# The context stage of a cross-attention kernel in written issue order, with the first group's keys and values taken together

## Chip, cores and metric

The kernel runs on one core of a Trainium2 chip. The metric is the device time of one execution in microseconds (us). The measurements are of whole executions; the profile is of one of them.

## The reference

Inputs are `x` (32 x 512 x 640), a context `ctx_2048` (32 x 77 x 1024) and weights `wq` (640 x 640), `wk` and `wv` (1024 x 640), `wo` (640 x 640) with a bias. Cut to what reaches the output:

```python
q = heads(x @ wq)                      # 20 heads of 32
k = heads(ctx @ wk); v = heads(ctx @ wv)    # 77 tokens per batch
p = softmax(einsum('bhqd,bhkd->bhqk', q, k) / sqrt(32))
out = merge(einsum('bhqk,bhkd->bhqd', p, v)) @ wo + bias + x
```

The reference also has key and value projections for object, other and image tokens. They take the context's tokens beyond the 77th, and there are none, so nothing of them reaches the output.

## The kernel before

Every float32 product is made of three products of halves: an operand is split into a high part (a copy rounded to `fp32r`, on ScalarE, ACT) and a low part (the operand less the high part, on VectorE, DVE, or on GpSimd, POOL), and `PAIRS` lists high x high, high x low and low x high. The helper `split` (L104 for the high part, L105 for the low) serves weights, context, keys and values, so many operations have its lines and are told apart by tile.

**The context stage.** The 32 x 77 = 2464 context tokens are worked in five groups of 512 (the last has 416). For a group, `load_context` loads its tokens (tile `cs`, L144, issued on SyncE's queue, SP), `context` transposes one chunk of 128 channels in 32 x 32 blocks on DVE (tile `craw`, L153) and splits it (tile `ct`, 9 buffers). There are `NK` = 8 such chunks. `keys` (L164) adds three matmuls of one chunk `k` for one block `j` of 128 key columns into a bank of PSUM (`pk`); there are `NC_` = 5 blocks, so a group has 120 matmuls for keys and, in `context_values` (L192, tile `pv`), 120 for values. A finished block of keys is split (`ks`, two buffers) and stored into `k_dram` (L177 and L179, issued on POOL, for the last group on SP). A finished block of values is transposed (`vt`, L200, one buffer), split (`vs`, two buffers) and stored into `v_dram` (L205, on SP).

`split_weights` loads one or two chunks of a weight (tile `wraw`, two buffers, L114) and splits them (`wk_s`, `wv_s`, `wq_s`). In group 0 it takes wk chunk by chunk with the context; wv is loaded after that, behind the keys; wq follows in group 1 and wo, which is stored split in `wo_dram`, in group 2. Twelve matmuls on a tile of zeros (`warm`, L237) run on TensorE (PE) before the first load has landed. The tile of zeros also fills the tail of `v_dram`.

In the last group the keys go block by block. Its values go later, as fillers beside the first slots of the main loop, and the first batch of `x` is loaded (`load_x`, tile `xs`), transposed (`transpose_x`) and split (`split_x`, tile `xt`, L228 and L229) in its time.

**Order.** Up to there, the order of the instructions on each engine is the tile framework's: its scheduler orders the program by a timeline that it works out itself, from the data flow, the buffers and its own costs. From `with tc.manual_schedule` near the end of the function on, the order on each engine is the written one. DMAs issued by one engine stand in that engine's order, too: a load whose buffer is not yet free holds up all that is issued behind it.

**The main loop.** It has N = 160 slots (32 batches x 5 blocks of 4 heads): `queries` (tile `pq`, L353), `split_q` (`qt`, L364 to L370), `scores` (`sc`, L388; `nm`, L396), exponentials (L406), normalisation and a transpose through DRAM, values (`pa`, L480) and the output projection (`po`, L510). It reads the keys back from `k_dram` (tiles `kb`, `kc`) and the values from `v_dram` (`vb`). Slots 0 and 1 have the last group's values beside them, through `psv`.

## Time and profile before

| | us |
|---|---|
| median of 3 runs | 1971.68 |
| their range | 1971.13 to 1974.15 |
| the profiled execution | 1971.65 |
| its span, first to last instruction | 1969.2 |
| busy in it: PE / ACT / DVE / POOL | 1932.0 / 1592.9 / 1362.1 / 1020.6 |
| mean granted clock of TensorE | 0.994 |

The profiled execution's time exceeds its span by 2.45 us, which lie before the first and after the last instruction. In a row of a timeline the columns are the start and the duration in us, the engine, the line, the operation, the tile written and the tiles read, shapes, the number of instructions taken together, and in brackets the idle time ahead of them with what ended it. In a row of the chain of waits they are start, duration and what the time went to. PEld is the load of weights into TensorE, which overlaps matmuls; SPq and POOLq are the issue of DMAs by SyncE and GpSimd. PEclk is the clock that TensorE was granted as a share of full speed; the DMA share is the mean busy share of the core's 16 DMA engines.

### The profile page before, as it was taken

The page shows a single profiled execution, that of the slowest core. Times are in us where ns is not written, and L with a number is a line of the kernel's source. Part 1 is how long each engine was busy: PE and PEld are TensorE (multiplying, and loading weights), DVE is VectorE, ACT ScalarE, POOL GpSimd, SP SyncE. Part 2 cuts the span into 40 slices and gives each one's busy share as a digit, 9 for nine tenths or more (in the row PEclk, how much of TensorE's full clock was granted, in tenths as well). Part 3 has the DMA queues.
Part 4 walks back from the last instruction along what each step waited for, and adds up shares of the span by engine and source line. Part 5 has one row for each costly group of instructions (what it writes and reads, how often), then busy time and mean ns, then how long its engine had stood idle before and what let it go on. Part 6 is the DMA issues. An engine that isn't in the chain of part 4 may idle for free.

```text
span 1969.2 us, 37571 instructions
## 1 busy us (share of the span) xinstructions
PE 1932.0 (98%) x10652; PEld 1729.6 (88%) x10652; DVE 1362.1 (69%) x2166; ACT 1592.9 (81%) x6362; POOL 1020.6 (52%) x680
## 2 busy tenths in 40 slices
PE   7999998899999999999999999999999999999999
PEld 5788897789999999999999999999999999999998
DVE  4544345777777777777777777777777777777774
ACT  2422147889999999999999999999999999999993
POOL 0111143565555555565556665566556655555555
PEclk9999999899999999999999999999999999999999
DMA  9996478888888888888888888988888888888876
GB/s 188 247 215 125 97 147 188 226 224 231 221 231 228 222 228 226 231 229 223 224 228 234 218 227 224 234 227 227 227 224 225 222 227 223 226 225 227 231 192 188
DMA packets 600698, 423.49 MB, mean 215 GB/s; under 512 B 219792, under 2 KB 509358, under 8 KB 600494
## 3 DMA queue, kind: packets, MB, share of 16 engines
q1 hardware_dynamic: 596973, 410.61, 82.5%
q0 software_dynamic: 3520, 10.49, 2.0%
q8 instruction: 88, 1.44, 0.3%
q14 instruction: 117, 0.95, 0.2%
HBM read 245.61 MB, written 175.32 MB: 214 GB/s over the span
## 4 chain that ended last, share of the span: by engine, by line
PE 89%; DMA 5%; SPq 2%; issue 1%; ACT 1%; POOL 1%; DVE 1%; POOLq 0%; DVEq 0%; ACTq 0%
PE po L510 28%; PE pq L353 27%; PE pa L480 14%; PE sc L388 10%; PE pv L192 6%; PE pk L164 5%; DMA cs<-in_ctx_dram 1%; DMA wo_s<-wo_dram 1%; DMA wraw<-in_L_xattn_to_v_w_dram 1%; DMA k_dram<-ks 1%; SPq L435 1%; DMA raw<-pd 1%; DMA pd<-z 1%; SPq L144 0%; POOL pn L421 0%
## 5 line engine op out<-in xcount | busy, mean ns | idle before, releaser
L406 ACT ACTIVATE pn<-sc,nm 128x77 f32<-128x77 f32 x2560 | 797.3, 328 | 48.2 <-DVE nm L396 33.3
L421 POOL TENSOR_TENSOR pn<-pn,rs 128x1232 f32<-128x1232 f32 x160 | 364.4, 2277 | 641.9 <-DVE rs L416 629.7
L510 PE MATMUL po<-wo_s,at 128*128 128x320 f32 x3840 | 625.9, 312 | 0.1
L353 PE MATMUL pq<-xt,wq_s 128*128 128x512 f32 x2400 | 618.9, 398 | 2.4 <-DVE ks L105 1.2
L510 PEld LDWEIGHTS po<-wo_s,at 128*128 128x128 f32 x3840 | 565.0, 188 | 0.7 <-DVE xr L538 0.3
L406 ACT ACTIVATION_READ_ACCUMULATOR pn<-sc,nm 128x1 f32 x2560 | 529.1, 207 | 0.0
L396 DVE TENSOR_REDUCE nm<-sc 128x4 f32<-128x308 f32 x640 | 294.3, 460 | 315.9 <-PE sc L388 311.4
L353 PEld LDWEIGHTS pq<-xt,wq_s 128*128 128x128 f32 x2400 | 427.9, 189 | 79.7 <-POOL xt L229 2.4
L480 PE MATMUL pa<-pp,vb 128*128 128x512 f32 x1280 | 329.1, 399 | 2.2 <-POOL pp L466 2.0
L480 PEld LDWEIGHTS pa<-pp,vb 128*128 128x128 f32 x1280 | 243.2, 197 | 41.3 <-POOL pp L466 3.4
L428 DVE STREAM_TRANSPOSE z<-pn 128x1280 f32<-128x1280 f32 x160 | 241.1, 1507 | 27.5 <-POOL pn L421 16.9
L459 DVE TENSOR_TENSOR pp<-raw,pp 128x1024 fp32r<-128x1024 f32 x160 | 196.3, 1227 | 64.0 <-ACT pp L452 56.7
L466 POOL TENSOR_TENSOR pp<-raw,pp 64x512 fp32r<-64x512 f32 x160 | 210.6, 1317 | 48.6 <-ACT pp L458 29.1
L388 PEld LDWEIGHTS sc<-kc,qt 128*128 128x128 f32 x1280 | 212.0, 189 | 24.1 <-ACT qt L368 3.8
L370 DVE TENSOR_TENSOR qt<-pq,qt 64x512 fp32r<-64x512 f32 x320 | 214.6, 670 | 16.1 <-ACT qt L364 11.7
L229 POOL TENSOR_TENSOR xt<-xs,xt 128x512 fp32r<-128x512 f32 x160 | 204.1, 1293 | 40.8 <-DMA k_dram<-ks 32.8
L388 PE MATMUL sc<-kc,qt 128*128 128x154 f32 x1280 | 222.8, 255 | 2.2 <-DVE qt L370 2.1
L388 PE MATMUL sc<-kb,qt 128*128 128x308 f32 x640 | 195.8, 306 | 11.7 <-ACT pn L406 6.3
L503 POOL TENSOR_TENSOR xr<-xr,bias 128x640 f32<-128x640 f32 x128 | 200.9, 1571 | 9.7
L368 ACT CAST qt<-qt 64x512 fp32r<-64x512 f32 x320 | 198.0, 619 | 9.0
L452 ACT CAST pp<-raw 128x1024 fp32r<-128x1024 f32 x160 | 170.1, 1063 | 13.6 <-DMA raw<-pd 12.5
L104 ACT CAST at<-pa 128x512 fp32r<-128x512 f32 x160 | 94.5, 591 | 80.0 <-PE pa L480 79.7
(43 smaller groups left out, 1537.5 us busy)
## 6 DMA issues: line engine op xcount, KB each, us to landing
pd<-z SPq DMA_DIRECT2D x640, 160.0 KB, 3.5
raw<-pd SPq DMA_DIRECT2D x160, 512.0 KB, 4.3
xs<-in_x_dram SPq DMA_DIRECT2D x128, 320.0 KB, 6.1
xr<-in_x_dram SPq DMA_DIRECT2D x128, 320.0 KB, 3.7
out_dram<-xr SPq DMA_DIRECT2D x127, 320.0 KB, 3.0
raw<-pd SPq DMA_DIRECT2D x160, 128.0 KB, 4.4
v_dram<-vs SPq DMA_DIRECT2D x80, 128.0 KB, 3.1
kc<-k_dram SPq DMA_DIRECT2D x128, 57.8 KB, 4.1
```

What stands on the lines that cost most here:

```text
L229: low.tensor_tensor(parts[1], src, parts[0].bitcast(F32), ALU.subtract)
L353: nc.tensor.matmul(pqs[n], wq_s[:, k, a, j * P : (j + 1) * P], xts[b, k][:, c, :], start=(k == 0 and m == 0), stop=(k == NC_ - 1 and m == 2),)
L370: nc.vector.tensor_tensor(qt[r, 1 + w, :], pq[r], qt[r, 0, :].bitcast(F32), ALU.subtract)
L388: nc.tensor.matmul(sc[:, cols], qt[:, m, t * P : (t + 1) * P], keys_, start=(m == 0), stop=(m == 2),)
L396: nc.vector.tensor_reduce(nm, sc[:, :KCOLS].rearrange("p (h k) -> p h k", k=NKEY), AX.X, ALU.max, negate=True)
L406: nc.scalar.activation(pnb[n % 2][:, at, :NKEY], sc[:, i * NKEY : (i + 1) * NKEY], AF.Exp, bias=nm[:, i : i + 1], accum_out=sms[n][:, at : ...
L421: nc.gpsimd.tensor_tensor(pf, pf, rs.unsqueeze(2).to_broadcast([P, NQ * HPC, NKEY]), ALU.mult)
L428: nc.vector.transpose(z.rearrange("p b t j -> p t b j"), pn.rearrange("p (t h) k -> p t (h k)", t=NQ).rearrange("p t (b i) -> p t b i", i=Q),)
L466: nc.gpsimd.tensor_tensor(pp[64:, 4, :], raw[:64, 2, :], pp[:64, 4, :].bitcast(F32), ALU.subtract)
L480: nc.tensor.matmul(pas[n], vb[:, t, :, a], pp[:, c, :], start=(m == 0), stop=(m == len(PASSES) - 1),)
L503: nc.gpsimd.tensor_tensor(xrs[b, t], xrs[b, t], bias, ALU.add)
L510: nc.tensor.matmul(pos[b, t, h][:, :HALF], ats[b * NC_ + j][:, a, t * P : (t + 1) * P], wos[0][:, j, c, h * HALF : (h + 1) * HALF], start= ...
```

## The change

The whole context stage moves into the manual schedule, so that each engine takes its instructions in the written order. The functions are cut into parts that can be ordered separately: `load_weights` from `split_weights`, `transpose_context` from `split_context`, `split_keys` from `keys`, `values_of` and `split_values` from `context_values`.

In group 0, `first` takes a chunk of channels at a time: its transpose and split, the split of wk, 15 matmuls for the five blocks of keys, the split of wv and 9 matmuls for the first three blocks of values. The eight banks of PSUM hold five blocks of keys and three of values. Value blocks 3 and 4 follow as 48 matmuls. The loads go out by turns: context, wk and wv of one chunk (later of two), half of the first wk on ACT's queue and the first two chunks of wv on POOL's.

From group 1 on, a group's context is one tile of 8 chunks with one buffer, loaded by four DMAs of 512 KB when the group before it has been transposed. Its first chunk is transposed and split at value block 1 of the group before, the others before value block 4 is split. All five `split_keys` of a group come after its keys; the splits of wq and wo stand between `vt` and `vs`. `wraw` has three buffers, and wq is scaled in place.

In the last group the keys are taken in two rounds, blocks 0 to 2 and then 3 and 4, with `x` of batch 0 loaded ahead of the last value block of group 3 and its transposes and splits ahead of the last group's `ks`. The number of matmuls is the same, and the order of the main loop too.

```diff
--- before.py
+++ after.py
-    def split_weights(dst, w, k0, kn=1, permuted=True, scale=None):
-        raw = kvw.tile([P, 2, C], F32, tag="wraw", name="wraw", bufs=2)[:, :kn]
+    def load_weights(w, k0, kn, permuted=True, queues=(nc.sync,) * 4, tag="wraw"):
+        raw = kvw.tile([P, 2, C], F32, tag=tag, name="wraw", bufs=3 if tag == "wraw" else 2)
         if permuted:
             rows = w.rearrange("(q c i) n -> q i c n", q=4, i=Q)
-            for q in range(4):
-                nc.sync.dma_start(raw[q * Q : (q + 1) * Q], rows[q, :, k0 : k0 + kn])
+            for q, queue in enumerate(queues):
+                queue.dma_start(raw[q * Q : (q + 1) * Q, :kn], rows[q, :, k0 : k0 + kn])
         else:
-            nc.sync.dma_start(raw[:, 0], w[k0 * P : (k0 + 1) * P, :])
+            rows = w.rearrange("(c p) n -> p c n", p=P)
+            nc.sync.dma_start(raw[:, :kn], rows[:, k0 : k0 + kn])
         for k in range(kn):
-            part = raw[:, k]
-            if scale is not None:
-                part = kvw.tile([P, C], F32, tag="wscaled", name="wscaled", bufs=1)
-                nc.scalar.mul(part, raw[:, k], scale)
-            split(dst[:, k, 0, :], dst[:, k, 1, :], part)
+            wraws[id(w), k0 + k] = raw[:, k]
+    def split_weights(dst, w, k, scale=None):
+        part = wraws.pop((id(w), k))
+        if scale is not None:
+            nc.scalar.mul(part, part, scale)
+        split(dst[:, 0, :], dst[:, 1, :], part)
...
-    kvc = tc.alloc_tile_pool(name="kvc", bufs=3, side="right")
+    kvc = tc.alloc_tile_pool(name="kvc", bufs=1, side="right")
...
-    def load_context(g0, gn, k0, kn):
+    cts, pks, pvs, css, craws, wraws = ({} for _ in range(6))
+
+    def load_context(g, *counts):
+
+        g0, gn = GROUPS_KV[g]
         src = ehs_flat[g0 : g0 + gn, :].rearrange("(a j) (q u) -> q j a u", j=Q, q=4)
-        cs = kvc.tile([P, G // Q, 4 * Q], F32, tag="cs", name="cs", bufs=3)
-        for q in range(4):
-            nc.sync.dma_start(
-                cs[q * Q : (q + 1) * Q, : gn // Q, : kn * Q],
-                src[q, :, :, k0 * Q : (k0 + kn) * Q],
-            )
-        for k in range(kn):
-            css[g0, k0 + k] = cs[:, : gn // Q, k * Q : (k + 1) * Q]
-
-    def context(g0, gn, k):
-        raw = kvt.tile([P, G], F32, tag="craw", name="craw")
+        if g not in css:
+            css[g] = kvc.tile([P, G // Q, NK * Q], F32, tag="cs", name="cs"), [0]
+        cs, done = css[g]
+        for kn in counts:
+            cols = slice(done[0] * Q, (done[0] + kn) * Q)
+            for q in range(4):
+                nc.sync.dma_start(
+                    cs[q * Q : (q + 1) * Q, : gn // Q, cols], src[q, :, :, cols]
+                )
+            done[0] += kn
+
+    def transpose_context(g, k):
+        gn = GROUPS_KV[g][1]
+        craws[k] = kvt.tile([P, G], F32, tag="craw", name="craw")
         nc.vector.transpose(
-            raw[:, :gn].rearrange("p (a j) -> p a j", j=Q), css.pop((g0, k))
+            craws[k][:, :gn].rearrange("p (a j) -> p a j", j=Q),
+            css[g][0][:, : gn // Q, k * Q : (k + 1) * Q],
         )
+
+    def split_context(g, k):
+        gn = GROUPS_KV[g][1]
         ct = kvp.tile([P, 2, G], FPR, tag="ct", name="ct", bufs=9)
-        split(ct[:, 0, :gn], ct[:, 1, :gn], raw[:, :gn])
-        cts.append(ct)
-
...
-    def keys(g0, gn, j, k):
+        split(ct[:, 0, :gn], ct[:, 1, :gn], craws.pop(k)[:, :gn])
+        cts[g, k] = ct
+
+    def context(g, *ks):
+
+        transpose_context(g, ks[0])
+        for k in ks:
+            if k + 1 in ks:
+                transpose_context(g, k + 1)
+            split_context(g, k)
+
+    def context_product(held, tag, g, j, k, w, pool):
+        gn = GROUPS_KV[g][1]
         if k == 0:
-            pks[j] = psk.tile([P, G], F32, tag="ps", name="pk")
+            held[j] = pool.tile([P, G], F32, tag="ps", name=tag)
         for n, (a, c) in enumerate(PAIRS):
             nc.tensor.matmul(
-                pks[j][:, :gn],
-                wk_s[:, k, a, j * P : (j + 1) * P],
-                cts[k][:, c, :gn],
+                held[j][:, :gn],
+                w[:, k, a, j * P : (j + 1) * P],
+                cts[g, k][:, c, :gn],
                 start=(k == 0 and n == 0),
                 stop=(k == NK - 1 and n == 2),
             )
-        if k == NK - 1:
-            pk = pks.pop(j)
-            ks = kvt.tile([P, 2, G], FPR, tag="ks", name="ks")
-            split(ks[:, 0, :gn], ks[:, 1, :gn], pk[:, :gn])
-            engine = nc.gpsimd if g0 != GROUPS_KV[-1][0] else nc.sync
-            dst = k_dram.rearrange("(h r) c w n -> r c w h n", h=2)[:, j, :, :, g0 : g0 + gn]
-            engine.dma_start(dst[:, 0].bitcast(F32), ks[:64, :, :gn].bitcast(F32))
-            for half in range(2):
-                engine.dma_start(
-                    dst[:, 1, half].bitcast(F32), ks[64:, 1 - half, :gn].bitcast(F32)
-                )
-
-    xts, xss, xpool = {}, {}, []
-
-    def context_values(g0, gn, j, pool):
-
-
+
+    def keys(g, j, k):
+        context_product(pks, "pk", g, j, k, wk_s, psk)
+
+    def split_keys(g, j):
+        g0, gn = GROUPS_KV[g]
+        ks = kvt.tile([P, 2, G], FPR, tag="ks", name="ks")
+        split(ks[:, 0, :gn], ks[:, 1, :gn], pks.pop(j)[:, :gn])
+        engine = nc.gpsimd if g + 1 < len(GROUPS_KV) else nc.sync
+        dst = k_dram.rearrange("(h r) c w n -> r c w h n", h=2)[:, j, :, :, g0 : g0 + gn]
+        engine.dma_start(dst[:, 0].bitcast(F32), ks[:64, :, :gn].bitcast(F32))
+        for half in range(2):
+            engine.dma_start(dst[:, 1, half].bitcast(F32), ks[64:, 1 - half, :gn].bitcast(F32))
+
...
+    def split_values(g, j, between=None):
+
+        g0, gn = GROUPS_KV[g]
...
         vt = kvp.tile([P, G], F32, tag="vt", name="vt", bufs=1)
-        nc.vector.transpose(vt[:, :gn], pv[:, :gn])
+        nc.vector.transpose(vt[:, :gn], pvs.pop(j)[:, :gn])
+        if between is not None:
+            between()
         vs = kvp.tile([P, G // Q, HD, 2], FPR, tag="vs", name="vs", bufs=2)
         split(vs[:, :na, :, 0], vs[:, :na, :, 1], vt[:, :gn].rearrange("p (a d) -> p a d", d=HD))
...
+    ctx.enter_context(tc.manual_schedule(engines=ENGINES))
+    zero = kvt.tile([P, 2, G], FPR, name="zero", tag="ks")[:, 0]
     nc.vector.memset(zero.bitcast(F32), 0.0)
     warm = psk.tile([P, G], F32, tag="ps", name="warm")
     for _ in range(12):
         nc.tensor.matmul(warm, zero[:, :P], zero, start=True, stop=True)
-    g0, gn = GROUPS_KV[0]
-    starts = {0: 1, 1: 1, 2: 2, 4: 4}
-    for k in range(NK):
-        if k in starts:
-            load_context(g0, gn, k, starts[k])
-        if k in (0, 1, 2, 4, 6):
-            kn = 1 if k < 2 else 2
-            split_weights(wk_s[:, k : k + kn], wk, k, kn)
-        context(g0, gn, k)
+    def first(*ks):
+        for k in ks:
+            transpose_context(0, k)
+        for k in ks:
+            split_context(0, k)
+            split_weights(wk_s[:, k], wk, k)
+            for j in range(NC_):
+                keys(0, j, k)
+            split_weights(wv_s[:, k], wv, k)
+            for j in range(3):
+                context_product(pvs, "pv", 0, j, k, wv_s, psk)
+    load_context(0, 1)
+    load_weights(wk, 0, 1, queues=(nc.scalar, nc.scalar, nc.sync, nc.sync))
+    load_weights(wv, 0, 1, queues=(nc.gpsimd,) * 4, tag="ws")
+    load_context(0, 1)
+    load_weights(wk, 1, 1)
+    load_weights(wv, 1, 1, queues=(nc.gpsimd,) * 4, tag="ws")
+    load_context(0, 2)
+    load_weights(wk, 2, 2)
+    first(0)
+    first(1)
+    load_weights(wv, 2, 2)
+    load_context(0, 4)
+    for k in range(2, NK, 2):
+        first(k, k + 1)
+        if k < 6:
+            load_weights(wk, k + 2, 2)
+            load_weights(wv, k + 2, 2)
+    nc.sync.dma_start(bias, bo.unsqueeze(0).to_broadcast([P, C]))
+    LAST, split_ks = len(GROUPS_KV) - 1, []
+    def split_wq():
+        k = len(split_ks)
+        split_ks.append(k)
+        split_weights(wq_s[:, k], wq, k, scale=SCALE)
+    def split_wo():
+        k = len(split_ks) - NC_
+        split_ks.append(k)
+        ws = kvw.tile([P, 2, C], FPR, tag="ws", name="ws", bufs=2)
+        split_weights(ws, wo, k)
+        nc.sync.dma_start(wo_dram[:, k].bitcast(F32), ws.bitcast(F32))
+    load_context(1, NK)
     nc.sync.dma_start(
         v_dram[NT:].rearrange("n i j d a -> (n i j d a)").rearrange("(p u) -> p u", u=P).bitcast(F32),
         zero[: (KPAD - NKEY) * HEADS * HD * 2 // P, :P].bitcast(F32),
     )
-    for g, (g0, gn) in enumerate(GROUPS_KV):
-        if g:
-            cts.clear()
-            for k in range(NK):
-                context(g0, gn, k)
-        if g == 0:
-            for k in range(0, NK, 2):
-                split_weights(wv_s[:, k : k + 2], wv, k, 2)
-            nc.sync.dma_start(bias, bo.unsqueeze(0).to_broadcast([P, C]))
-        if g + 1 < len(GROUPS_KV):
-            for k0 in range(0, NK, 4):
-                load_context(*GROUPS_KV[g + 1], k0, 4)
-        else:
-            kvw.release()
-            kvc.release()
-            xpool.append(
-                ctx.enter_context(tc.tile_pool(name="xpool", bufs=1, reuse_waits="tile"))
-            )
-            load_x(0)
-            for i in range(NQ):
-                transpose_x(0, i)
-            for c in range(NC_):
-                split_x(0, c)
-            load_x(1)
-        if g + 1 < len(GROUPS_KV):
+    for g in range(LAST):
+        for j in range(NC_):
+            if g or j > 2:
+                values_of(g, j, psk)
+            if not g and j < 3:
+                split_keys(0, j)
+            if not g and j == 2:
+                continue
+            if j == 1:
+                context(g + 1, 0)
+            if not g and j == 3:
+                split_values(0, 2)
+                split_keys(0, 3)
+            if j == NC_ - 1:
+                if not g:
+                    context(g + 1, 1, 2)
+                    split_keys(0, 4)
+                context(g + 1, *range(1 if g else 3, NK))
+                if g + 1 == LAST:
+                    kvw.release()
+                    kvc.release()
+                    xpool.append(
+                        ctx.enter_context(
+                            tc.tile_pool(name="xpool", bufs=1, reuse_waits="tile")
+                        )
+                    )
+                    load_x(0)
+            split_values(g, j, (None, split_wq, split_wo, None)[g])
+        if g + 1 < LAST:
+            load_context(g + 2, NK)
+            if g < 2:
+                for k in range(0, NC_, 2):
+                    load_weights((wq, wo)[g], k, min(2, NC_ - k), permuted=g == 0)
             for k in range(NK):
                 for j in range(NC_):
-                    keys(g0, gn, j, k)
-        else:
+                    keys(g + 1, j, k)
             for j in range(NC_):
-                for k in range(NK):
-                    keys(g0, gn, j, k)
-        if g0 == GROUPS_KV[1][0]:
-            for k in range(0, NC_, 2):
-                kn = min(2, NC_ - k)
-                split_weights(wq_s[:, k : k + kn], wq, k, kn, scale=SCALE)
-        if g0 == GROUPS_KV[2][0]:
-            for k in range(NC_):
-                ws = kvw.tile([P, 1, 2, C], FPR, tag="ws", name="ws", bufs=1)
-                split_weights(ws, wo, k, permuted=False)
-                nc.sync.dma_start(wo_dram[:, k].bitcast(F32), ws[:, 0].bitcast(F32))
-        if g0 != GROUPS_KV[-1][0]:
-            for j in range(NC_):
-                context_values(g0, gn, j, psk)
+                split_keys(g + 1, j)
+    for i in range(NQ):
+        transpose_x(0, i)
+    for c in range(NC_):
+        split_x(0, c)
+    for round_ in (range(3), range(3, NC_)):
+        for k in range(NK):
+            for j in round_:
+                keys(LAST, j, k)
+        for j in round_:
+            split_keys(LAST, j)
+        if j == 2:
+            load_x(1)
...
-    with tc.manual_schedule(engines=ENGINES):
...
```

## The prediction

> **What bounds the kernel now.** I read the page first: PE is busy 98% of the span, and the only slices of the 40 in which it is clearly not are at the start and around the seventh and eighth. Then the chain of waits over 0–520 us, because it names what ends last in each stage:
>
> ```profile
> 41.95 7.14 DMA wraw<-in_L_xattn_to_v_w_dram
> 49.11 7.41 DMA wraw<-in_L_xattn_to_v_w_dram
> 57.39 22.77 PE pv L192 x92
> 80.16 27.20 PE pk L164 x120
> 107.36 27.20 PE pv L192 x120
> 243.36 8.97 PE pk L164 x48
> ```
>
> To be seen: until 57.39 us the chain runs through loads, after it through matmuls alone: 120 matmuls in 27.20 us, 0.2267 us each, for every half of a group until the last group (its 416 columns take 22.56). Nothing that DVE, ACT or a DMA does between 80.16 and 265 us costs time; only the stretch before 80.16 and the few microseconds after 265 can give any. The timeline of PE over 0–82 us shows the stretch:
>
> ```profile
> 7.52 7.42 PE L164 MATMUL pk<-ct,wk_s 128*128 128x512 f32 x30 [0.67 <-ACT wk_s L104]
> 17.71 7.14 PE L164 MATMUL pk<-ct,wk_s 128*128 128x512 f32 x30 [2.77 <-ACT wk_s L104]
> 26.16 13.91 PE L164 MATMUL pk<-ct,wk_s 128*128 128x512 f32 x60 [1.31 <-ACT wk_s L104]
> 45.44 5.80 PE L192 MATMUL pv<-ct,wv_s 128*128 128x512 f32 x13 [5.37 <-ACT wv_s L104]
> 51.55 3.71 PE L192 MATMUL pv<-ct,wv_s 128*128 128x512 f32 x15 [0.31 <-ACT wv_s L104]
> 57.39 22.77 PE L192 MATMUL pv<-ct,wv_s 128*128 128x512 f32 x92 [2.12 <-ACT wv_s L104]
> ```
>
> The 240 matmuls of group 0 need 240 x 0.2267 = 54.4 us and take 80.16 − 7.52 = 72.6. Of the 18.2 us too much, 2.77 + 1.31 + 5.37 + 0.31 + 2.12 = 11.9 are idle; the other 6.3 are matmuls that ran slow after a gap (13 in 5.80 us are 446 ns each) or dribbled in with their chunk. ACT is only the last hand in these waits: the waits view puts ACT itself behind the load of wv. The stretches by time show what the loads achieve:
>
> ```profile
> core 0: us, PE busy (x) PEld busy (x) DVE busy (x) ACT busy (x) POOL busy (x), PEclk, DMA share, GB/s
> 15.00:20.00 5.00, 2.29 (x10) 1.88 (x11) 3.57 (x5) 2.29 (x4) 0.00 (x0) 1.00 1.20 192
> 30.00:35.00 5.00, 5.00 (x24) 4.14 (x23) 2.15 (x3) 1.34 (x3) 0.00 (x0) 1.00 1.22 186
> 40.00:45.00 5.00, 0.07 (x1) 0.00 (x0) 0.00 (x0) 0.34 (x1) 0.00 (x0) 0.91 1.14 207
> 45.00:50.00 5.00, 4.57 (x11) 3.43 (x12) 2.16 (x3) 1.49 (x3) 1.82 (x3) 0.50 1.13 202
> 55.00:60.00 5.00, 2.88 (x9) 2.08 (x8) 2.16 (x3) 2.43 (x4) 0.80 (x3) 0.78 0.74 221
> ```
>
> The DMA share is at or over 1 where PE idles: the DMA engines are full, at 186–207 GB/s. And at 40–45 us they are full of the wrong thing: group 1's context (2.1 MB, issued 24.6–45 us) goes between wk and wv, so wv's first chunks land at 44.66 and its last at 59.4, though PE has done with the keys at 40.1.
>
> **The change part by part.** The profiled execution took 1971.65 us (span 1969.2, 2.45 around it); the median of the runs is 1971.68. The sum is made against 1971.65.
>
> *Group 0 by chunks of channels.* Same matmuls, another order: 24 per chunk (15 of keys, 9 of the first three blocks of values), then 48 for value blocks 3 and 4. Each chunk needs 256 KB of context and 320 KB each of wk and wv, 917 KB in bytes. At the 200 GB/s of those rows that is 4.6 us per chunk against 24 x 0.2267 = 5.44 us of PE, so PE becomes the slower side after a lead-in. My landings: each wk or wv pair 2.8 us (in before such a pair, 655 KB, landed 16.93 − 14.06 = 2.87 and 25.38 − 22.60 = 2.78 after the context ahead of it), the 1.05 MB of cs4–7 5.7 us (as before). Chunk 0 at 7.8 us, chunk 1 at 13, context of 2–3 at 16.5–17, wk 2–3 at 19.7, wv 2–3 at 22.5, context 4–7 at 28.2, wk 4–5 at 31.0, wv 4–5 at 33.8, wk 6–7 at 36.7, wv 6–7 at 43–44 (this last one is issued only once a wraw buffer is free, about 37.4). PE: chunks 0 and 1 from 7.5 to 18.4; a wait of some 2 us for wk 2; chunks 2 and 3 20.4–31.3; a wait of 0.4; chunks 4 and 5 to 42.6; 6 and 7 to 53.5; the last 48 matmuls to 64.4.
>
> *The clock.* Rows: after 2.77 us of idle, 30 matmuls took 7.14 us (238 ns, no loss to speak of); after 5.37, 13 took 5.80, with a granted clock of 0.50 in 45–50 us. So a gap of about 2 us is on the cheap side and 5 on the dear one. [...] By the rows, compute per chunk (5.44) is above the load (4.6), so there are one or two gaps and not eight. I take 1.4 us for one cold start (13 matmuls at 0.1–0.2 us too much), 0 to 6.7 as ends. Group 0 then ends at 65.8.
>
> *Loads on three issuing engines.* Half of wk 0 goes out on ACT, wv 0 and 1 on POOL. In before the first eight loads go out on SP between 0.74 and 4.65 us, about 0.5 us each. [...] I take 0 (ends −1 and +1).
>
> *Group 0 to group 1.* Group 1's context is no longer a stream that delays wv. It goes out last, as one tile with one buffer: 4 loads of 512 KB that can be issued only after the transposes of chunks 6 and 7 (about 41–43 us). Queue position: all of group 0's bytes (7.34 MB), bias and its 2.1 MB are 9.77 MB, at 200 GB/s after the first 6 us done at 54.5–55.5. Behind it on SP stand the zero fill of v_dram, and later v_dram's own stores. On DVE the transpose of group 1's chunk 0 stands ahead of what value blocks 0–2 and keys 3–4 still need from DVE; if cs is late, these wait in order behind it. From there DVE works its chain (16 context instructions at about 0.7 us, five ks, one vt and vs): chunk 1 of group 1 is ready near 68.7–70 against a need at 65.8 + 3.4 = 69.2, a stall of 0–1; I take the keys' effective start as 66.0. Against 80.16: **14.2 us**.
>
> *Groups 1 to 3.* The context of the next group is transposed and split during the values, its chunk 0 at block 1 and the rest before block 4; ks come all together behind the keys instead of being mixed. Counting DVE (0.7 us each) from the start T of the values: ks done by T + 10.6, chunk 1 of the next group by about T + 26, needed at T + 27.2 + 3.4 = T + 30.6. 4.5 us of slack, and DVE is busy only 66.8 of 163.2 us here, so it hides, as do the splits of wq and wo between vt and vs. If this cover were gone, each switch would cost what the chain is late, 0–1.5 us each, three times. Taken: 0.
>
> *End of the stage.* x(0) is now loaded before the last value blocks of group 3 and its transposes and splits stand ahead of the last group's ks on DVE and ACT. In before PE waits 1.22 us at 266.98 (for ks). After: the queries have xt in time, that wait goes; next is the load of kb and kc, which needs all k_dram stores: landed about 35.4 us after the last group's keys start against PE there at 35.0. Gain 1.2 − 0.4 = **0.8**; ends −3.5 (ks late behind x(0)) and 1.2.
>
> *Main loop.* Its order and instructions stay; the DMA-bound stretch around 308–357 us moves along. 0.
>
> Sum: 14.2 + 0.8 = 15.0; 1971.65 − 15.0 = 1956.7, **1957 us**.
>
> **The rivals.**
> 1. *Chunks fed one by one.* Loads at the 186 of the 30–35 us row or less, a wait before every pair of chunks and a lowered clock after it. Group 0 ends near 72, gain about 8: **1964**. For: the data of chunks 2–7 are never more than 3 us ahead at first. Against: 5.44 against 4.6 us. Chance 0.14.
> 2. *The last group's ks behind x(0).* ACT and DVE run in order, ks waits for the 6.1 us x load and 9 instructions more, the load of kb and kc comes 4 us late: **1961**. Against: x(0) goes out ahead of block 4's stores, about when the last group's keys start, and the queries need xt 22.6 us later. Chance 0.09.
> 3. *Slower: group 1's context, one buffer, last in the queue.* DVE stops at its transpose, and keys of group 1 stop with it. Each microsecond of landing after 54.5 costs one. The gain is gone when it lands at 69–70, that is at a mean of 140–147 GB/s in place of 200. Such a rate is in before (256-byte pieces of context, 0.52 MB in the 3.5 us of that stretch, at about 147); at 140 with the ring's waits it lands at 72, and the time is **1974.5**. For: SP, with at most eight loads in flight, stands in front of it; against: every 5 us row at this point shows 186 or more, and these pieces are 1 KB. Chance 0.05, and 0.02 more for other harm of that size.
> 4. *No change*: chunk order only shifts the wait for wv, which lands last in any case. It would need wv to land at 59 again; the 2 MB now behind it speak against. 0.02.
>
> **How the numbers follow.** The forecast has 0.68, and its own range is 1953–1961 (from a feed with no cold clock, and group 0 at its 54.4 us, to 4 us of stalls at the switches). With rivals 1 and 2 the range is **1951–1966**; left out are rival 3, no change, and part of rival 1. The measurement can tell about 0.2%, 3.9 us, from no change. Faster by more: forecast, rivals 1 and 2, 0.91; within: 0.02; slower: 0.07.
>
> **What would show it.** In the profile after: keys and values mixed on PE from about 7.5 us with one wait of about 2 us before chunk 2, group 0's matmuls ending at 64–67 and not 80; wv's last load landing near 44 and cs of group 1 near 55; group 1's keys starting near 66; halves of 27.20 us without idle to the last group; queries without the 1.22 us wait. Wrong if PE waits before every pair of chunks with a granted clock near 0.5 (rival 1), if sc waits for kb (rival 2), if DVE's transposes of group 1 wait for cs beyond 60 us (rival 3), or if the main loop after 410 us takes another length than before.

## The result and the profile after

The changed kernel takes 1958.06 us (median of 6 runs, 1955.52 to 1962.78) against 1971.83 for the kernel before measured beside it (6 runs): a ratio of 0.9931, 95% interval 0.9916 to 0.9947, some 13.8 us less. The forecast was 1957 in 1951 to 1966. The profiled execution is the longest of the six: 1962.78, span 1960.8, clock 0.995. So the two profiles differ by 8.9 us where the medians differ by 13.8; what lies between is taken up below.

The timeline of PE, start to the switch to group 1 (columns as explained under the table of times before):

```profile
9.18 5.70 PE L186 MATMUL pk<-ct,wk_s 128*128 128x512 f32 x15 [2.23 <-ACT wk_s L104]
...
52.80 13.08 PE L186 MATMUL pv<-ct,wv_s 128*128 128x512 f32 x57
65.72 3.56 PE L186 MATMUL pk<-ct,wk_s 128*128 128x512 f32 x15
70.76 0.50 PE L186 MATMUL pk<-ct,wk_s 128*128 128x512 f32 x1 [1.48 <-ACT ct L104]
71.49 10.77 PE L186 MATMUL pk<-ct,wk_s 128*128 128x512 f32 x39 [0.22 <-DVE ct L105]
```

Group 0 is one unbroken run of matmuls from 9.18 to 65.72, where group 1's keys start. The same view of the kernel before has them at 80.00 (the 80.16 of the prediction is the end of the last matmul of group 0, 65.88 here):

```profile
80.00 27.36 PE L164 MATMUL pk<-ct,wk_s 128*128 128x512 f32 x120
```

But PE starts 1.66 us later than before (7.52), the first 15 matmuls take 5.70 us and not the 3.56 of the later chunks, and after the first chunk of group 1 there is a wait. A second wait of the same form stands at the switch to group 3:

```profile
178.43 3.56 PE L186 MATMUL pk<-ct,wk_s 128*128 128x512 f32 x15
183.66 0.49 PE L186 MATMUL pk<-ct,wk_s 128*128 128x512 f32 x1 [1.67 <-ACT ct L104]
184.39 25.48 PE L186 MATMUL pk<-ct,wk_s 128*128 128x512 f32 x104 [0.23 <-DVE ct L105]
```

104 matmuls at 0.2267 are 23.6 us; here they take 25.48, and 25.50 at group 1. The stretches by time behind the first wait tell why:

```profile
72.00:73.00 1.00, 1.00 (x4) 0.81 (x4) 1.00 (x3) 0.00 (x0) 0.07 (x1) 0.67 0.94 157
73.00:74.00 1.00, 1.00 (x4) 0.72 (x3) 0.85 (x2) 0.66 (x2) 1.00 (x2) 0.50 1.07 220
...
75.00:76.00 1.00, 1.00 (x4) 0.77 (x4) 1.00 (x2) 0.47 (x1) 0.00 (x0) 0.62 0.66 197
```

PEclk, the third column from the end, is at one half for about 3.4 us (72.3 to 75.8): PE is busy throughout, but in the trace a matmul starts every 0.427 us there, and every 0.23 before and after. (The count in brackets takes in every matmul that touches the stretch.) So each switch costs not 1.7 to 1.9 but 3.9 (96.83 − 65.72 − 27.2) and 4.1 us (209.71 − 178.43 − 27.2).

What stands ahead of the ct (the split context) that PE waited for at group 1 is seen in the chain of waits:

```profile
41.90 13.26 DMA v_dram<-zero
...
62.76 5.15 DMA v_dram<-vs
68.01 0.66 ACT vs L104
...
70.74 0.70 DVE ct L105
71.49 25.50 PE pk L186 x104
```

ct of chunk 1 is behind the fourth block's vs in the written order of ACT and DVE (on ACT that vs starts at 68.01 us and the ct at 70.09), and that vs waits until a store to v_dram has landed (at 67.91) and freed one of its two buffers. The zero fill stands in the chain with 13.26 us; whether it held anything is tested below.

### The profile page after: what moved, and what is told of

Same layout as the page of the kernel before. It is cut to its first block, busy times and chain, and to the rows that moved or that the text cites. A ratio compares the mean times of both kernels' runs of the same rounds, so it can differ in the third digit from the quotient of the medians.

```text
span 1960.8 us, 37536 instructions
## 1 busy us (share of the span) xinstructions
PE 1933.2 (99%) x10652; PEld 1730.5 (88%) x10652; DVE 1362.5 (69%) x2166; ACT 1601.0 (82%) x6362; POOL 1024.4 (52%) x688
## 3 DMA queue, kind: packets, MB, share of 16 engines
q8 instruction: 88, 1.44, 0.3%
## 4 chain that ended last, share of the span: by engine, by line
PE 84%; DMA 7%; SPq 2%; ACT 2%; DVE 2%; issue 1%; POOL 1%; ACTq 0%; DVEq 0%; POOLq 0%
PE po L583 28%; PE pq L426 26%; PE pa L553 14%; PE sc L461 10%; PE pk L186 4%; PE pv L186 3%; DMA raw<-pd 2%; DMA pd<-z 1%; ACT pn L479 1%; DMA xs<-in_x_dram 1%; DMA v_dram<-zero 1%; DMA k_dram<-ks 1%; SPq L224 1%; POOL pn L494 1%; DMA wraw<-in_L_xattn_to_k_w_dram 0%
```

## The experiments

Twelve runs in three groups, each timed beside the kernel before (medians 1971.23 for e1 to e4, 1970.77 for e5 to e8, 1970.12 for e9 to e12). These differ by 1.1 us, so a microsecond between medians of different groups says nothing; each ratio is to the kernel before of the same group. Theory 1 is that the gain is group 0's loads in the right order, with waits at the start and at two switches taking part of it back. The rivals are in the expectations.

**e1_ct_first.** The two chunks of context that PE needs next go ahead of the blocked vs, in every group:

```diff
+            if j == 3:
+                continue
             if j == NC_ - 1:
+                context(g + 1, 1, 2)
+                split_values(g, 3, (None, split_wq, split_wo, None)[g])
                 if not g:
-                    context(g + 1, 1, 2)
                     split_keys(0, 4)
-                context(g + 1, *range(1 if g else 3, NK))
+                context(g + 1, *range(3, NK))
```

> The changed kernel with one move: chunks 1 and 2 of the next group's context are transposed and split ahead of the fourth block's values (vt, vs) and not behind them. Theory 1 (the two waits of about 1.7 us at the switches to groups 1 and 3, each with some 2 us of slow matmuls behind it, come from DVE and ACT standing in order at vs and ws, whose buffers wait for stores): both waits go, 104 matmuls no longer stand apart from the first 15, the first keys of the last group come 4 to 8 us earlier than in the changed kernel's profile (236.91), and the time is 1950 to 1954. Rival (the stage is held by its stores, and what PE gains is given back where the scores wait for kb and kc): the switches are clean but the scores of slot 0 start no earlier than 270, time 1957 to 1959.

Measured: 1957.81 (1954.46 to 1958.87), ratio 0.9931 (0.9917 to 0.9944). Both waits are gone, and the last group's keys start at 229.73 and not 236.91. Yet the time is that of the changed kernel. The timeline of PE:

```profile
229.73 22.56 PE L186 MATMUL pk<-ct,wk_s 128*128 128x416 f32 x120
268.07 0.60 PE L464 MATMUL sc<-kb,qt 128*128 128x308 f32 x1 [3.31 <-POOL vb L397]
```

7.2 us forward at 229.73, 4.7 at the first scores (268.07 against 272.79): a wait of 3.31 us has come, with the clock lowered behind it (0.72 in 265 to 270 us, 0.60 in 270 to 275). The theory holds for the cause of the waits and misses the time (1950 to 1954). The rival has the time, as the gain is given back at the scores, though these start before its 270.

**e7_ct_first3.** The same for the groups before the last alone; at group 3 the order stays, so that x is not pushed behind one more block of values.

```diff
+            if j == 3 and g + 1 < LAST:
+                continue
             if j == NC_ - 1:
-                if not g:
+                if g + 1 < LAST:
                     context(g + 1, 1, 2)
+                    split_values(g, 3, (None, split_wq, split_wo, None)[g])
+                if not g:
                     split_keys(0, 4)
-                context(g + 1, *range(1 if g else 3, NK))
+                context(g + 1, *range(3 if g + 1 < LAST else 1, NK))
```

> As e1_ct_first, but only for the groups before the last: at group 3's values the order stays as in the changed kernel, so that the first batch of x is loaded as early as there. Theory 1 (in e1 the clean switches brought the last group's keys 7.2 us forward, and 2.5 us of wait and 2 us of slow matmuls before the first scores came back because x went out behind one more block of values): keys of the last group at 229 to 230.5, first scores 35.9 us later, at 265 to 266.5, time 1952 to 1955.5. Rival (the DMA queues at the end of the stage hold the scores whatever the order): first scores at 267 to 269 again, time 1956 to 1959.

Measured: 1953.28 (1952.05 to 1954.08), ratio 0.9907 (0.9891 to 0.9924). The timeline of PE has keys of the last group at 229.04 and first scores 35.6 us later:

```profile
229.04 22.56 PE L186 MATMUL pk<-ct,wk_s 128*128 128x416 f32 x120
264.60 0.38 PE L465 MATMUL sc<-kb,qt 128*128 128x308 f32 x1 [0.52 <-DVE xs L246]
```

Theory 1 has the keys and the time right; the scores come 0.4 us ahead of its range (265 to 266.5). In the changed kernel x is issued at 236.08, 0.83 us before the last group's keys; in e1 at 231.80, 2.07 after; here at 228.21, again 0.83 before. Where x is issued set the wait in e1.

**e8_x_early.** As e7, with x ahead of the last two blocks of group 3's values.

```diff
-            if j == 3 and g + 1 < LAST:
+            if j == 3:
                 continue
...
                     load_x(0)
+                    split_values(g, 3)
```

> As e7_ct_first3, and x of batch 0 is loaded ahead of the last two blocks of group 3's values and not of the last one alone. Theory 1 (the first scores wait for kb and kc, these for the last group's ks, and ks for PE, not for x): x lands 3 us or more earlier but the first scores start within 0.5 us of e7's, time 1952 to 1956. Rival (x is what holds ks): ks and the first scores come 1 to 2.5 us earlier than in e7, time 1950 to 1953.5.

Measured: 1951.63 (1949.70 to 1952.41), ratio 0.9896 (0.9882 to 0.9911). x is issued at 223.76, 4.45 us earlier, and the first scores start at 264.36, 0.24 earlier, of which 0.21 stood there already when the keys began (228.83). So theory 1 holds on what the scores wait for: an earlier x does not bring them forward. The time lies just under its range and in the rival's, but the intervals of e7 and e8 overlap, so the medians don't tell the two apart.

**e9_zero_wo.** Two suspects, at two places: the zero fill, issued ahead of group 1's context load, and the five splits of wo (tile `ws`) with their stores, moved behind all of group 2's values. The second edit:

```diff
-            split_values(g, j, (None, split_wq, split_wo, None)[g])
+            split_values(g, j, (None, split_wq, None, None)[g])
+            if g == 2 and j == NC_ - 1:
+                for _ in range(NC_):
+                    split_wo()
```

> The changed kernel with two edits that act at different places: the zero fill of v_dram is issued ahead of group 1's context load, and the five splits of wo stand behind all of group 2's values and not between their vt and vs. Theory 1 (the switch to group 1 is held by vs's two buffers and their stores, and the chain names the zero fill only because it landed at that moment; the switch to group 3 is held by ws, whose two buffers wait for the stores to wo_dram, and by vs behind it): the switch to group 1 keeps a wait of 0.5 to 1.7 us at the second chunk, the switch to group 3 has none; the last group's keys start 2 to 4 us earlier than in the changed kernel's profiles (233.3 to 236.9); time 1954 to 1958. Rival (the zero fill, landing at 55 us, holds the buffers of ks and so all of DVE's chain): no wait at group 1 either, time 1952 to 1955. Rival for the second switch (v_dram's stores alone hold vs there): the wait at group 3 stays at 1 us or more.

Measured: 1960.31 (1959.68 to 1964.51), ratio 0.9956 (0.9939 to 0.9972). The timeline of PE settles both:

```profile
71.42 0.50 PE L186 MATMUL pk<-ct,wk_s 128*128 128x512 f32 x1 [1.59 <-ACT ct L104]
...
179.05 27.36 PE L186 MATMUL pk<-ct,wk_s 128*128 128x512 f32 x120
273.43 0.38 PE L464 MATMUL sc<-kb,qt 128*128 128x308 f32 x1 [4.17 <-ACT vs L104]
```

The wait at group 1 stays (1.59): the zero fill is innocent, though the chain gave it 13.26 us; it landed when the next instruction was due anyway. The wait at group 3 is gone without wo's splits in the values: they, with their stores, were its cause. Which of the buffers of ws and vs held it more is not separated; in the changed kernel's chain the longest piece there is a store of ws (172.81, 6.33 us). The time was missed. In the trace the stores of wo keep SP from 193.53 to 204.77, the last group's context is issued behind them at 204.82 (196.91 in the changed kernel), and x goes out at 236.21, 2.76 us after the last group's keys have begun. As in e1, the chain ahead of the first scores then runs through the loads of x, and the wait there is 4.17 us.

**e2_sp_start.** The changed kernel with the first loads all on SP's queue.

```diff
-    load_weights(wk, 0, 1, queues=(nc.scalar, nc.scalar, nc.sync, nc.sync))
-    load_weights(wv, 0, 1, queues=(nc.gpsimd,) * 4, tag="ws")
+    load_weights(wk, 0, 1)
+    load_weights(wv, 0, 1, tag="ws")
...
-    load_weights(wv, 1, 1, queues=(nc.gpsimd,) * 4, tag="ws")
+    load_weights(wv, 1, 1, tag="ws")
```

> The changed kernel with the first loads all on SP's queue: wk 0 not half on ACT's, wv 0 and wv 1 not on POOL's but behind wk 0 and wk 1. Theory 1 (the eight early loads of wv take the DMA engines from the context and wk of chunk 0, so PE starts at 9.18 us and cold): keys start at 7.5 to 8.0, the first 15 matmuls take 3.4 to 4.2 us and not 5.70, perhaps a wait under 1 us at chunk 1; group 0 ends at 62 to 64 and the time falls by 2 to 4 us, to 1954 to 1956. Rival (the bytes are the bound, so the order within the first two chunks only moves the wait): a wait of 1.5 to 3 us at chunk 1 takes the place of the late start, group 0 ends at 65 to 66, time as the changed kernel's 1958.

Measured: 1960.86 (1958.97 to 1965.41), ratio 0.9955 (0.9942 to 0.9967): the rival, with the wait at chunk 2 and not at chunk 1. The timeline of PE:

```profile
7.65 4.10 PE L186 MATMUL pk<-ct,wk_s 128*128 128x512 f32 x15 [1.31 <-ACT wk_s L104]
21.29 5.70 PE L186 MATMUL pk<-ct,wk_s 128*128 128x512 f32 x15 [2.06 <-ACT wk_s L104]
```

PE starts 1.5 us earlier, waits 2.06 for chunk 2 and finds the clock lowered there in place of the start (0.76 in 21 to 24 us, 0.67 in 24 to 27). Group 0 ends at 66.95, 1.2 us later. This start and this wait are what the forecast had for the changed kernel itself.

**e10_wv1_sp.** e8 with wv 1 alone moved back to SP's queue.

```diff
-    load_weights(wv, 1, 1, queues=(nc.gpsimd,) * 4, tag="ws")
+    load_weights(wv, 1, 1, tag="ws")
```

> e8_x_early with wv 1 loaded on SP's queue behind wk 1 and not on POOL's at the start; wv 0 stays on POOL's. Theory 1 (the 640 KB that POOL sends out between 1.3 and 5.4 us delay chunk 0, half of them half as much): keys start at 8.0 to 8.6 in place of 9.06, the wait ahead of them falls under 2 us and chunk 2 waits under 0.5 us; group 0 ends 0.3 to 1.5 us earlier, time 1950 to 1951.5. Rival (every byte taken off the start comes back at chunk 2, as in e2): a wait of 0.5 to 2 us at chunk 2, time 1951.5 to 1954.

Measured: 1954.02 (1950.69 to 1956.96), ratio 0.9919 (0.9905 to 0.9933): no gain. The keys start at 8.95 against 9.06: theory 1 missed. The transpose of the first context starts at 5.18 us in the kernel before, at 6.69 here and at 6.83 to 7.20 in the profiles with both chunks on POOL (7.01 in e8). So half of POOL's early bytes delays it hardly less; and what PE waits for by the chain is wk 0, which lands at 8.08 here and at 8.19 in e8. No wait came at chunk 2 either, so the rival is not shown; group 0 ends at 65.51 against e8's 65.63, and the first scores stand at 263.58, 0.8 ahead of e8. What moves the median by 2.4 us up is open: it lies behind the first scores, where this profile takes 3.9 us more than e8's, with 3.4 us more at half clock; and the intervals overlap.

**e11_warm20.** e8 with more warming matmuls.

```diff
-    for _ in range(12):
+    for _ in range(20):
         nc.tensor.matmul(warm, zero[:, :P], zero, start=True, stop=True)
```

> e8_x_early with 20 warming matmuls in place of 12, so that PE is busy until some 8.8 us and not 6.95. Theory 1 (the 2.1 us that the first 15 matmuls take too long are the granted clock at 0.5 for 3.4 us, brought on by PE's 2 us of idle before them, not late data): keys still start at 9.0 to 9.3, the first 15 take 3.4 to 3.9 us and not 5.7, group 0 ends 1.5 to 2.2 us earlier unless chunk 2 or 4 waits for its data, time 1949 to 1950.5. Rival (the first 15 run at the pace at which wk's low half and DVE come): still 5 us or more for them at a granted clock of 1.0, time as e8_x_early's 1951.6.

Measured: 1949.98 (1948.24 to 1953.98), ratio 0.9901 (0.9886 to 0.9917), within the noise of e8's but the lowest median here. The timeline of PE:

```profile
1.46 6.24 PE L264 MATMUL warm<-zero 128*128 128x512 f32 x20 [1.46 <-DVE zero L261]
9.02 4.11 PE L186 MATMUL pk<-ct,wk_s 128*128 128x512 f32 x15 [1.32 <-ACT wk_s L104]
```

4.11 us for the first 15 and not 5.71, from the same start, and the record of the granted clock has no half clock ahead of 332 us: the clock, not the data. Group 0 ends at 63.99, 1.64 us earlier than in e8 (65.63).

**e3_keys_first and e4_keys_turns.** The changed kernel with group 0's products in the order of the kernel before, keys and then values; in e3 wv's loads go behind wk's, in e4 the loads stay by turns.

```diff
             for j in range(NC_):
                 keys(0, j, k)
-            split_weights(wv_s[:, k], wv, k)
-            for j in range(3):
-                context_product(pvs, "pv", 0, j, k, wv_s, psk)
...
+    for k in range(NK):
+        for j in range(3):
+            context_product(pvs, "pv", 0, j, k, wv_s, psk)
```

> The changed kernel with group 0's products in the order of the kernel before: all keys chunk by chunk, then the values; wv's loads go out behind wk's but still ahead of group 1's context. Theory 1 (the gain is that group 1's 2 MB no longer stand ahead of wv): keys end near 40 to 41 as before, wv has landed by 42, values follow with a wait of 0 to 2 us, group 0 ends at 67 to 70, time 1958 to 1963. Rival (the gain is that keys and values of a chunk stand together on PE, so that PE does not wait chunk by chunk and stays at its clock): group 0 ends at 76 to 80, time 1969 to 1973.

> The changed kernel with its loads by turns as they are, but group 0's products in the order keys, then values. Now PE has 3.4 us of work per chunk against some 4.6 us of loads. Theory 1: PE waits about 1.2 us per chunk on the mean, keys end where wk 6 and 7 have landed, at 42 to 47, values follow without a wait, group 0 ends at 70 to 75 and the time is 1963 to 1968: worse than keys first with wk's loads first. If turns help by themselves: group 0 ends at or before 68, time 1958 to 1960. If gaps at every chunk also lower the clock: keys take over 42 us and the time is 1970 or more.

Measured: e3 1963.86 (1959.05 to 1965.16), ratio 0.9962 (0.9950 to 0.9975); e4 1968.85 (1964.81 to 1970.49), ratio 0.9988 (0.9979 to 0.9996). The timeline of PE of e3:

```profile
25.52 14.28 PE L186 MATMUL pk<-ct,wk_s 128*128 128x512 f32 x60 [1.00 <-ACT wk_s L104]
39.63 27.36 PE L186 MATMUL pv<-ct,wv_s 128*128 128x512 f32 x120
```

With wv right behind wk the values follow the keys without a wait, and group 0 ends at 66.83, 1.1 us behind the changed kernel: the waits for wv were group 1's context. The median of e3 is just past theory 1's range (to 1963) and far from the rival's. In e4 PE waits 1.56, 1.67 and 2.16 us for wk's chunks and group 0 ends at 78.25, beyond theory 1's 70 to 75: loads by turns are only worth having with products by turns. Its time is a little beyond theory 1's range and below that of the case in which every gap lowers the clock. In the trace that case holds in part: the clock is lowered behind the late start (45 matmuls in 13.89 us, where 45 at 0.2267 are 10.2) and behind the waits of 1.67 (45 in 13.24) and 2.16 us (0.66 in 45 to 50 us), but not behind the wait of 1.56 (1.00 in 25 to 30).

**e12_keys_first8.** e8, where the switches are clean, with the diff of e3.

> e8_x_early (clean switches) with group 0's products and loads as in e3_keys_first: all keys, then the values, wv's loads behind wk's and ahead of group 1's context. This prices the mixing of keys and values alone. Theory 1 (mixing gave 1.1 us in the profiles of e3_keys_first and the changed kernel; most of the 6 us between their medians are the switches' waits and lowered clocks): group 0 ends at 66.5 to 67.5, no or little wait at group 1, time 1951.5 to 1954. Rival (mixing is worth the 6 us of the medians, through later work that it leaves better placed): time 1956 to 1959, with a wait at the switch to group 1 that the clean order doesn't cover.

Measured: 1955.54 (1955.23 to 1957.51), ratio 0.9929 (0.9916 to 0.9943), between the two expectations. Group 0 ends at 67.08, 1.45 us behind e8, with a clean switch; the first scores stand at 265.55, 1.2 behind. The median is 3.9 behind. The profiles place 1.2 us of it ahead of the first scores and 2.6 behind them, where e12's has 3.4 us more at half clock. So mixing keys and values, with the order of the loads that goes with it, gives 1.2 to 3.9 us, and why the later part moves is open.

**e6_before_sp.** The kernel before with one thing: SP's order is the written one while group 0 is issued.

```diff
+    order = ExitStack()
+    order.enter_context(tc.manual_schedule(engines={mybir.EngineType.SP}))
     g0, gn = GROUPS_KV[0]
...
+        if g == 1:
+            order.close()
```

> The kernel before with one thing alone: while group 0 is issued, SP's queue takes its loads in the written order (wv's 16 loads right behind wk's and the zero fill, group 1's context behind them); all else stays with the framework's scheduler. Theory 1 (what the change gains is that group 1's context no longer stands ahead of wv): wv's last load lands by 42 to 44 and not 59.4, group 0 ends at 67 to 70, a clean switch to group 1, time 1958 to 1962. Rival (it takes the chunks of keys and values together, or the written order on the other engines): group 0 ends at 74 or later, or a wait of several us for group 1's context takes the place; time 1966 or more.

Measured: 1967.90 (1965.47 to 1971.37), ratio 0.9984 (0.9975 to 0.9993). Theory 1 holds for group 0, and the rival for the time and for the wait that takes the gain back. The timeline of PE:

```profile
40.44 27.30 PE L192 MATMUL pv<-ct,wv_s 128*128 128x512 f32 x117
...
76.69 27.24 PE L164 MATMUL pk<-ct,wk_s 128*128 128x512 f32 x105 [4.85 <-ACT ct L104]
```

Group 0 ends at 67.58, 12.4 us sooner than before (80.00). Then the keys of group 1 wait: counted back from the values at 103.76, they are where an unbroken half begun at 76.56 would be, so 9 of the 12.4 us are lost in one place. The chain of waits names it:

```profile
62.01 6.62 DMA wraw<-in_L_xattn_to_q_w_dram
...
75.39 0.74 ACT wscaled L121
76.13 0.52 ACT ct L104
76.69 27.24 PE pk L164 x105
```

The framework's order has scalings and splits of wq ahead of group 1's second chunk of context on ACT and DVE, and wq's load comes behind that context. Before, PE was late enough for that order to cost nothing. It is the other half of the change, the written order on ACT and DVE, that keeps the gain: in part in the changed kernel, where this switch loses 3.9 or 1.5 us, and in full in e7, where it loses none.

**e5_again.** The changed kernel unchanged, for a second profile.

> The changed kernel once more, unchanged, to see another execution of it: its profiled one took 1962.78 where the median was 1958.06. Theory 1 (a wait of 1 to 2 us costs itself, and in some executions some 2 us more because the granted clock falls to 0.5 for about 4 us after it; start and both switches stand such waits): times between 1955 and 1963 with a median of 1956 to 1960, waits at the same places in the profile (start, group 1, group 3), and in each of them either the 15 or 104 matmuls behind it at 227 to 240 ns each or some 2 us too much. Rival (the spread comes from the main loop's DMA): waits and clock at the start and the switches as in the first profile, and the difference behind 310 us.

Measured: 1957.48 (1956.77 to 1960.10), ratio 0.9931 (0.9917 to 0.9944); the profiled execution took 1960.10. The timeline of PE:

```profile
70.36 0.51 PE L186 MATMUL pk<-ct,wk_s 128*128 128x512 f32 x1 [0.66 <-ACT ct L104]
71.08 23.88 PE L186 MATMUL pk<-ct,wk_s 128*128 128x512 f32 x104 [0.22 <-DVE ct L105]
...
182.34 23.89 PE L186 MATMUL pk<-ct,wk_s 128*128 128x512 f32 x104 [0.22 <-DVE ct L105]
```

The waits stand at the same places, 0.66 and 1.65 us, but the 104 matmuls behind each take 23.9 us: the clock stayed up (1.00 from 70 to 76 us). The first scores come at 269.19 and not 272.79, and behind them the two profiles differ by 0.9 us the other way. The two switches together cost 4.1 us less here, the start 0.4 more. So the 2.7 us between these two executions come from the switches, as theory 1 has it.

## Why the prediction was right, and where it was not

The time (1957 for 1958.06) came out for the reason named: wv no longer waits behind group 1's context, PE runs through group 0, and the end of group 0 moves from 80.00 to 65.72 (forecast 65.8). e3 and e6 show that the order of the loads alone does nearly all of that: 13.2 and 12.4 of the 14.3 us. But terms of the sum were off and partly made up for each other, and that the median lies 1 us from the forecast is in part luck: the sum starts from a profiled execution, and the profiled ones after took 1962.78 and 1960.10, 6.1 and 3.4 us over its 1956.7.

- **Group 0's parts.** Forecast: start at 7.5, a wait of 2 us before chunk 2, 1.4 us of lowered clock. Measured: start at 9.18, 2.1 us too much in the first 15 matmuls, no wait at chunk 2 and none of 0.4 behind it. So 1.7 and 0.7 us more and 2.4 us less cancel. The late start took up the wait; e2, which starts at 7.65, has the wait (2.06).
- **The clock.** A gap of about 2 us was put on the cheap side. A row that the prediction shows speaks against it: 55 to 60 us, behind the wait of 2.12 us, has a clock of 0.78, and the 92 matmuls there took 22.77 us in place of 20.9. After, a lowered clock followed waits of 1.48 to 2.23 us too. No run shows the 6.7 us at the upper end of this term: in the changed kernel's group 0 a lowered clock followed one wait and cost 2.1 us; in e4 it followed three of four.
- **Loads on three issuing engines**, taken at 0 with ends −1 and +1, which were my estimate and which no run shows: the start was 1.66 us later, beyond the end that I gave. e3 and e12, with wk 0 half on ACT as here but no early wv on POOL, have the first transpose at 5.88 and 5.99 us (7.13 here) and the first keys at 7.92 and 8.04 (9.18 here), so most of the 1.66 us is wv's. It came back later as the wait not had, so that undoing it in e2 gained nothing (2.8 us lost in the medians, with intervals that just overlap).
- **Group 0 to group 1**, a stall of 0 to 1, taken at 0.2: 3.9 and 1.5 us in the two profiles. The load that the step looked at was on time (zero fill behind it landed at 55.16; forecast for the context 54.5 to 55.5), so rival 3's trigger was absent. I counted durations on DVE, 0.7 us each, and not the buffers: vs has two, a store took 5.15 us to land, and DVE stood 4.04 us at one vs. e1 and e7 remove the wait by the order alone, and e9 clears the zero fill.
- **Groups 1 to 3**, taken at 0: none at groups 2 and 4, but 4.1 and 2.5 us at group 3. I had put wo's splits under "hides" on DVE's busy share; what I left out are their stores on SP, and that ws has two buffers as well. e9 shows that the splits and stores are the cause, the chain that the stores are waited for. DVE's busy share, 67 in 163 us, did not show these waits: in the changed kernel ACT stood 2.73 us for a store of vs and 2.22 us for one of ws, and DVE 2.56 and 1.44 us behind it.
- **End of the stage**, 0.8: from the last group's keys to the first scores 36.4 us before, 35.9 after. Gain 0.5; here the reading held, and e1 and e9 show rival 2's mechanism, a late x in front of ks and of the loads behind it, at 3.3 and 4.2 us of wait.
- **Main loop**, taken at 0: span less first scores is 1689.6 before, 1688.0 and 1688.9 after, 1685.3 in e8. The difference goes the way of the time at half clock behind the first scores (13.7 us before, 10.2 in both profiles after, 6.8 in e8); that the clock is the cause is not shown, since PE also waits there.

The first scores, before and after:

```profile
279.56 0.30 PE L388 MATMUL sc<-kb,qt 128*128 128x308 f32 x1
272.79 0.38 PE L461 MATMUL sc<-kb,qt 128*128 128x308 f32 x1 [0.84 <-DVE vt L217]
```

There the profiles are 6.8 and 10.4 us ahead (e5 has 269.19) where the sum had 15.0; the forecast without its two missed switches is what e7 and e8 measure (264.60 and 264.36 against 279.56 − 15.0 = 264.6), with 1953.28 and 1951.63 for the time. That is 3.4 and 5.1 us under the 1956.7, and in their profiles the main loop is 4.1 and 4.3 us shorter than before. That the medians of the changed kernel lie nearer to the forecast than its profiles may be the clock in part: its shortest two executions, 1955.52 and 1955.99, have a mean clock of 0.997 and the profiled ones 0.995, but one of 1957.46 has 0.994. What these executions did at the switches no trace shows.

## What to carry to other kernels

When a load order is put right, look next at what the old wait had hidden: here the order of instructions on ACT and DVE, which gave back 9 us where it was left to the framework and some 4 to 8 where it was written with stores in front of the next group's inputs. Put the instruction that feeds the bound engine ahead of any that waits for a buffer, as e1 and e7 did (waits of 1.48 and 1.67 us gone), and cost each such buffer by its store's time to land (here 5.15 us for vs and 6.33 for ws), not by the engine's busy share. A name in the chain of waits is a suspect: here the zero fill had a row of 13.26 us, and with it moved ahead of the context load the wait stayed (1.59 us).

## What the runs showed of the hardware

In the profiles before and after, the trace's record of the granted clock has only 1.00 and 0.50. Its stretches at 0.50 in the first 420 us last 6.83, 3.41, 3.41 and 10.24 us before, and four times 3.41 and once 6.83 after. Waits of PE, the row behind them and the clock, from several profiles:

```
wait, us        matmuls behind it              at half clock   busy share of PE in the
                                               behind it       3.41 us ahead of the fall
2.77 (before)   30 in 7.14                     none            -
2.12 (before)   92 in 22.77                    3.41 us         0.38
2.23 (after)    15 in 5.70                     3.41 us         0.47
1.48 (after)    104 in 25.50                   3.41 us         0.50
1.67 (after)    104 in 25.48                   3.41 us         0.44
1.65 (e5)       104 in 23.89                   none            -
1.48 (e3)       104 in 23.91                   none            -
1.32 (e11)      15 in 4.11                     none            -
2.06 (e2)       15 in 5.70, before chunk 2     3.41 us         0.36
```

So a wait of 1.3 to 2.8 us costs itself, and in some of these profiles 1.6 to 2.1 us more: there the wait was charged twice, and 1.48 us was enough for it. The same wait at the same place does either from one execution to the next (the switch to group 3: 25.48 us behind 1.67 in the changed kernel, 23.89 behind 1.65 in e5).

The length of the wait alone does not tell the two apart: 2.77 us in the kernel before had no half clock behind it, 1.48 us had it after and not in e3. Nor does the share of PE alone: 0.45 in the 3.41 us from 13.42 to 16.83 before, which hold most of the wait of 2.77, was followed by no half clock; 0.47 and 0.50 in the table were. What decides is not shown.
